# Expert tiles of 128 slots in place of 256 for the first three images of a deformable-convolution and mixture-of-experts block

## The chip, the cores and the metric

The kernel runs on one core of a Trainium2 chip. The metric is the device time of one execution in microseconds (us). Before the change it is 7743.53 us, the median of 9 runs between 7716.26 and 7766.05 us.

## The reference

The input is four images of 256 channels and 64 by 64 pixels, in 32-bit floats, as all arithmetic is.

```python
x = x + conv_ref(ln_c(x))        # three modulated deformable 3x3 convolutions, each with relu
t = to_tokens(x)                 # 4 images x 4096 tokens x 256
t = t + ffn_ref(ln_t(t))         # 8 experts, the two best of each token

# a deformable layer: an ordinary 3x3 convolution gives 9 offsets and masks a pixel,
# the input is sampled there bilinearly, and the 9 samples are contracted:
sampled = bilinear(x, ys, xs) * mask
out = einsum('bikhw,oik->bohw', sampled, wk) + b

# the experts:
probs = softmax(xf @ gate_w + gate_b);  top2_vals, top2_idx = top_k(probs, 2)
cw = zeros(N, 8).at[arange(N), top2_idx].add(top2_vals)
for e in range(8):
    out += cw[:, e] * (gelu(xf @ W1[e] + b1[e]) @ W2[e] + b2[e])   # 256 -> 512 -> 256
```

## The kernel before

The convolutions come as twelve stages, one for each layer and image (`run`, L1018). A stage is eight blocks of 512 pixels, and a block is nine taps, one for each place of the 3x3 kernel: 864 taps in all. For a tap, `samples` (L476) has POOL issue four indirect gathers of 128 rows (tile `g`), VectorE (DVE) blends each in two steps (L491, L496, tile `s`), and ScalarE (ACT) scales it (L499). `turn` (L503) has TensorE (PE) transpose the four results, eight transpositions into two PSUM tiles `tp` (L514), and ACT copy each half into `sT` (L517). `finish` (L523) then contracts `sT` with the tap's weights into `acc` (L537): four products of 512 columns. A 32-bit product is two passes on PE, and each pass is one record in the trace with a weight load of its own; a transposition is one pass.

Ten buffers hold `g` and eight hold `s`, so that POOL and DVE can run ahead of PE. The code calls `turn` two pairs of samples behind `samples`.

The experts of an image run beside later taps. `tokens` finds each token's two experts, `route` (L671) gives every token-and-expert pair a slot, sorted by expert, and fills the tables `tok` (which token is in a slot) and `wrow` (the rows of the weights of a tile). An expert's slots are rounded up to whole tiles. A `Group` is one image, or half of the last one: three groups of 39 tiles of 256 slots (`FT`, L36), and two of 23. `expert` (L806) does one tile in three pieces:

1. the tokens `zt`, 128 rows a DMA, are transposed into a `tp` tile (`ftp`, L821), and ACT copies it to `fzT` (L825);
2. the first products (`ph`, L837), in two halves that share one PSUM tile, and after each half two Gelus on ACT (`hT`, L847), a Gelu reading its bias from the weights' buffer;
3. the second products (`py`, L855). At the start of the next tile's first piece `products` (L864) adds the bias on DVE (`y`, L873) and stores the result by SP's queue.

`fetch` (L771) issues a tile's weights and then its tokens on POOL's queue. It is called in the third piece of the tile before (L851), behind the newest gather; while lanes are drained, in the second piece (L830). Of the weights there are two buffers, used in turn. The tiles are taken alternately from the first and the second half of a group (`order`, L86), so that each buffer walks the experts in order, and a request whose rows are those already in the buffer gets row numbers out of bounds: it is issued, but moves nothing (L733 to L737).

When a piece's turn comes is set by `Lane.go`: every tap gives a credit of one, and a piece of a tile costs a third of its group's pace (L1030), 5, 5, 2, 1.5 and 0 taps a tile. What is still left in the lanes after the last tap is drained.

This is the order in which the kernel's code names the work. A scheduler of the tile layer then orders the instructions of each engine, by a model of its own of when each can start; the engines run them in that order. `after` ties an instruction behind another one.

Of the kernel before, what the change touches and what calls it, by code (L numbers as in the profile page):

```python
# [33 lines left out]
HC = HID // P  # L34
FT_LOG = 8
FT = 1 << FT_LOG  # L36
FU = FT // P
GB = 10
# [34 lines left out]
class Group:  # L73


    def __init__(self, b, n0, n1):
        self.b, self.n0, self.n1 = b, n0, n1
        self.nm = f"{b}_{n0}"
        self.M = (n1 - n0) * TPB

        self.NF = 2 * self.M * P // FT + E - 1


        self.half = (self.NF + 1) // 2
        self.zt, self.acc, self.gy, self.sums, self.py = {}, [], [], [], None
        self.order = [s // 2 + s % 2 * self.half for s in range(self.NF)]  # L86
# [21 lines left out]
class Weave:  # L108
# [96 lines left out]
    def ffn_constants(self):  # L205
# [7 lines left out]
        ]  # L213
        nf = max(g.NF for g in self.groups)
        for g in self.groups:
            g.zd = self.dram.tile([g.M * P, C], F32, name=f"z_{g.nm}", tag=f"z_{g.nm}")
        self.ys = [
            self.dram.tile([nf * FT, C], F32, name=f"ys_{i}", tag=f"ys_{i}") for i in range(3)
        ]
# [40 lines left out]
        nc.vector.tensor_copy(self.row_f, row_i)  # L260
        assert FU * nf <= P
        self.token = cst.tile([P, NB * TPB], F32, name="token")
# [408 lines left out]
    def route(self, grp):  # L671

        nc, M, NF = self.nc, grp.M, grp.NF
        grp.slots = self.rt2.tile([P, 2, M], I32, tag="slots", bufs=3, name=f"slots_{grp.nm}")
        grp.tok = self.rt2.tile([P, FU * NF], I32, tag="tok", name=f"tok_{grp.nm}")
        grp.wrow = self.rt2.tile([P, NF], I32, tag="wrow", name=f"wrow_{grp.nm}")
# [19 lines left out]
        ni = small("ni", (P, E), I32)  # L696
        nc.vector.tensor_scalar(ni, slot[:, :, M - 1], float(FT - 1), None, ALU.add)
        nc.vector.tensor_scalar(ni, ni, FT_LOG, None, ALU.logical_shift_right)
        nt = small("nt", (P, E))
# [4 lines left out]
        nc.vector.tensor_tensor(off, end, nt, ALU.subtract)  # L704
        nc.vector.tensor_scalar(off, off, float(FT), None, ALU.mult)
        nc.vector.tensor_tensor(slot, slot, tot, ALU.subtract)
# [34 lines left out]
        for v, (op, k) in enumerate(((ALU.bitwise_and, P - 1), (ALU.logical_shift_right, 7))):  # L741
# [4 lines left out]
            grp.digits.append(df)  # L746
        grp.inv = self.ps1.tile([P, FU * NF], F32, tag="py", name=f"inv_{grp.nm}")

    def invert(self, grp, m):
# [3 lines left out]
        lo, hi = grp.digits  # L753
        n = FU * grp.NF
        for i in range(2):
# [15 lines left out]
    def fetch(self, grp, step):  # L771

        if self.w is None:
            self.w = [
                self.wt.tile([P, 2, WINN], F32, tag="wt", name=f"w_{i}").rearrange(
                    "p a b -> p (a b)"
                )
                for i in range(2)
            ]
        f = grp.order[step]  # L780
        self.nc.gpsimd.indirect_dma_start(  # L781
            out=self.w[step % 2][:, : W1N + W2N],
            out_offset=None,
            in_=self.ins["W"],
            in_offset=bass.IndirectOffsetOnAxis(ap=grp.wrow[:, f : f + 1], axis=0),
            bounds_check=E * P - 1,
            oob_is_err=False,
        )
        grp.zt[step] = []
        for u in range(FU):  # L790
            zt = self.ffn.tile([P, C], F32, tag=f"zt{u}", name=f"zt_{grp.nm}_{f}_{u}")
            j = FU * f + u
            self.nc.gpsimd.indirect_dma_start(  # L793
                out=zt,
                out_offset=None,
                in_=grp.zd,
                in_offset=bass.IndirectOffsetOnAxis(ap=grp.tok[:, j : j + 1], axis=0),
            )
            grp.zt[step].append(zt)

    def fetch_next(self, grp, step):
        if step + 1 < grp.NF:
            with self.after(self.gathered):
                self.fetch(grp, step + 1)

    def expert(self, grp, step):  # L806

        nc = self.nc
        if step == 0:
            self.fetch(grp, 0)  # L810
            yield
        self.products(grp)
        f = grp.order[step]
        nm = f"{grp.nm}_{f}"
        w = self.w[step % 2]
        w1, w2 = w[:, :W1N], w[:, W1N : W1N + W2N]
        zt = grp.zt.pop(step)
        tp = self.ps.tile([P, CC, FT], F32, tag="tp", name=f"ftp_{nm}")
        for u in range(FU):
            for c in range(CC):  # L820
                nc.tensor.transpose(  # L821
                    tp[:, c, u * P : (u + 1) * P], zt[u][:, c * P : (c + 1) * P], self.ident
                )
        zT = self.ffn.tile([P, CC, FT], F32, tag="zT", bufs=1, name=f"fzT_{nm}")
        nc.scalar.copy(zT, tp)  # L825
        yield

        beside = not self.draining
        if not beside:
            self.fetch_next(grp, step)  # L830
        hT = []
        for h0 in range(0, HC, 2):
            ph = self.ps1.tile([P, 2, FT], F32, tag="ph", name=f"ph_{nm}_{h0}")
            for h in range(2):
                for c in range(CC):
                    o = c * HID + (h0 + h) * P
                    nc.tensor.matmul(  # L837
                        ph[:, h, :],
                        lhsT=w1[:, o : o + P],
                        rhs=zT[:, c, :],  # L840
                        start=(c == 0),
                        stop=(c == CC - 1),
                    )
            ht = self.ffn.tile([P, 2, FT], F32, tag="hT", bufs=3, name=f"hT_{nm}_{h0}")
            for h in range(2):
                k = CC * HID + h0 + h
                nc.scalar.activation(ht[:, h, :], ph[:, h, :], AF.Gelu, bias=w1[:, k : k + 1])  # L847
            hT.append(ht)
        yield
        if beside:  # L850
            self.fetch_next(grp, step)  # L851
        py = self.ps1.tile([P, FU, C], F32, tag="py", name=f"py_{nm}")
        for u in range(FU):
            for h in range(HC):
                nc.tensor.matmul(  # L855
                    py[:, u, :],
                    lhsT=hT[h // 2][:, h % 2, u * P : (u + 1) * P],
                    rhs=w2[:, h * C : (h + 1) * C],
# [5 lines left out]
    def products(self, grp):  # L864
# [5 lines left out]
        grp.py = None  # L870
        y = self.ffn.tile([P, FU, C], F32, tag="y", name=f"y_{grp.nm}_{f}")
        with self.after(self.last):
            nc.vector.tensor_tensor(  # L873
                y, py, w2[:, HC * C :].unsqueeze(1).to_broadcast([P, FU, C]), ALU.add
            )
        nc.sync.dma_start(
            self.ys[grp.i % 3][f * FT : (f + 1) * FT, :].rearrange("(u p) c -> p u c", u=FU),
            y,
# [137 lines left out]
    def run(self):  # L1016
# [9 lines left out]
        last = self.B - 1  # L1026
        self.groups = [Group(b, 0, NB) for b in range(last)]
        self.groups += [Group(last, 0, NB // 2), Group(last, NB // 2, NB)]

        for i, (g, pace) in enumerate(zip(self.groups, (5.0, 5.0, 2.0, 1.5, 0.0))):  # L1030
            g.i, g.pace, g.last = i, pace, i + 1 == len(self.groups)
# [82 lines left out]
```

## Time and profile before

| | us |
|---|---|
| median of 9 runs | 7743.53 |
| profiled execution | 7722.13 |
| its span, first to last instruction | 7720.4 |
| PE busy | 6511.4 (84%) |
| DVE busy | 4878.4 (63%) |
| POOL busy | 4445.1 (58%) |
| ACT busy | 3464.2 (45%) |
| first products `ph`, PE busy, 2608 passes of 256 columns | 700.9 |
| second products `py`, PE busy, 2608 passes of 256 columns | 673.7 |
| weight requests on POOL, 163 | 177.2 |
| token requests on POOL, 326 | 330.7 |

The stretches that the text speaks of, in us from the span's start: 1236 to 2429 are taps with no tiles beside them, 2429 to 4075 hold the first group's 39 tiles, 4248 to 5879 the second's, 6091 to 6851 most of the third's, and from 7286 on no tap is left.

A row of a group of instructions reads: line, engine, operation, out<-in, shapes, count | busy us, mean ns of one | idle time of the engine just before them, with what ended it. "PEld" is PE's weight load, which overlaps the products. A row of waits reads: who waited <- for whom: us in total, times, longest us. The clock is the share of TensorE's clock that was granted.

### The profile page before, as it was taken

How to read it: one execution, taken by the hardware profiler on the slowest of the kernel's cores; microseconds unless marked ns; L12 is line 12 of the kernel's file. 1: busy time of each engine (PE TensorE's matmuls, PEld its weight loads, DVE VectorE, ACT ScalarE, POOL GpSimd, SP SyncE). 2: the span in 40 equal slices, each digit the busy share in tenths (PEclk: the TensorE clock that was granted, in tenths of full speed). 3: DMA queues.
4: the chain of work that ended last, by engine and by line, in shares of the span. 5: the costliest groups of instructions: out<-in, count | busy, mean ns of one | idle time of the engine just before them, and what ended most of it. 6: DMA issues, size and time to landing. Idle time of an engine off the chain costs nothing.

```text
span 7720.4 us, 89391 instructions
## 1 busy us (share of the span) xinstructions
PE 6511.4 (84%) x26756; PEld 3635.2 (47%) x26756; DVE 4878.4 (63%) x10829; ACT 3464.2 (45%) x7381; POOL 4445.1 (58%) x4245
## 2 busy tenths in 40 slices
PE   7888888888888888888887888888878788977887
PEld 3343333334444444545544444444444455644665
DVE  5666777767787666667667556666667654567421
ACT  4454444445554444445553434444544333444322
POOL 4554666655556656655546656665556655556543
PEclk8999999999999999999998989999989999989998
DMA  7887999988898888888778878888888877778643
GB/s 255 294 296 283 349 338 337 349 332 319 314 327 314 308 295 300 306 297 303 277 289 293 285 272 314 299 303 300 280 293 294 280 256 240 273 273 299 226 140 121
DMA packets 802369, 2223.77 MB, mean 288 GB/s; under 512 B 106776, under 2 KB 304920, under 8 KB 796128
## 3 DMA queue, kind: packets, MB, share of 16 engines
q0 software_dynamic: 551200, 1947.35, 70.9%
q1 hardware_dynamic: 250688, 270.69, 10.4%
q8 instruction: 217, 3.56, 0.2%
q14 instruction: 264, 2.16, 0.1%
HBM read 2160.68 MB, written 196.40 MB: 305 GB/s over the span
## 4 chain that ended last, share of the span: by engine, by line
PE 64%; ACT 10%; another core or an unknown queue 9%; issue 7%; DVE 4%; DMA 2%; POOL 1%; ACTq 0%; SPq 0%; DVEq 0%; POOLq 0%
PE acc L537 32%; PE tp L514 10%; PE ph L837 6%; PE py L855 6%; PE po L341 5%; ACT sT L517 4%; ACT s L499 3%; DVE g L491 2%; DVE s L496 1%; PE pm L355 1%; ACT hT L847 1%; PE tpv L315 1%; PE ftp L821 1%; ACT win L559 1%
## 5 line engine op out<-in xcount | busy, mean ns | idle before, releaser
L485 POOL DMA_INDIRECT g<-tab,idx x3456 | 3650.8, 1056 | 2531.6 <-DVE s L496 1199.9
L537 PE MATMUL acc<-sT,wk 128*128 128x512 f32 x6912 | 3543.9, 626 | 313.9 <-ACT sT L517 162.6
L491 DVE SCALAR_TENSOR_TENSOR g<-g,cf 128x512 f32<-128x512 f32 x3456 | 2560.6, 743 | 277.6 <-DMA g<-tab,idx 221.6
L496 DVE SCALAR_TENSOR_TENSOR s<-g,cf 128x256 f32<-128x256 f32 x3456 | 1662.6, 483 | 1376.0 <-PE tp L514 734.9
L517 ACT COPY sT<-tp 128x512 f32<-128x512 f32 x1728 | 1003.0, 585 | 2388.5 <-PE tp L514 1545.6
L514 PE MATMUL tp<-ident,s 128*128 128x128 f32 x6912 | 1312.7, 288 | 542.3 <-ACT s L499 319.8
L514 PEld LDWEIGHTS tp<-ident,s 128*128 128x128 f32 x6912 | 891.9, 146 | 1839.0 <-issue 948.0
L537 PEld LDWEIGHTS acc<-sT,wk 128*128 128x128 f32 x6912 | 1204.3, 200 | 1141.5 <-issue 839.8
L499 ACT ACTIVATE s<-s,cf 128x256 f32<-128x256 f32 x3456 | 1631.9, 507 | 233.1 <-DVE s L496 163.3
L837 PE MATMUL ph<-fzT,w 128*128 128x256 f32 x2608 | 700.9, 402 | 88.5 <-ACT fzT L825 32.2
L855 PE MATMUL py<-w,hT 128*128 128x256 f32 x2608 | 673.7, 398 | 116.3 <-ACT hT L847 78.6
L837 PEld LDWEIGHTS ph<-fzT,w 128*128 128x128 f32 x2608 | 493.7, 200 | 235.2 <-issue 82.3
L855 PEld LDWEIGHTS py<-w,hT 128*128 128x128 f32 x2608 | 487.6, 197 | 240.8 <-ACT hT L847 112.2
L847 ACT ACTIVATE hT<-ph,w 128x256 f32<-128x256 f32 x652 | 284.2, 470 | 606.1 <-PE ph L837 352.8
L793 POOL DMA_INDIRECT zt<-z,tok x326 | 330.7, 1014 | 162.9 <-issue 90.5
L781 POOL DMA_INDIRECT w<-in_W,wrow x163 | 177.2, 1087 | 390.3 <-issue 149.8
L341 PE MATMUL po<-win,wo 128*32 128x504 f32 (+1 forms) x2304 | 374.5, 612 | 3.4 <-ACT win L295 2.7
L896 POOL DMA_INDIRECT gy<-ys,slots x256 | 262.8, 1026 | 104.9 <-issue 71.0
L873 DVE TENSOR_TENSOR y<-py,w 128x512 f32<-128x512 f32 x163 | 111.9, 686 | 311.2 <-PE py L855 271.2
L911 DVE SCALAR_TENSOR_TENSOR ta<-gy,cw,ta 128x256 f32<-128x256 f32 x256 | 120.5, 480 | 114.1 <-DMA gy<-ys,slots 60.3
L318 ACT COPY hv<-tpv 128x512 f32<-128x512 f32 x192 | 112.6, 587 | 174.8 <-remote 75.0
L341 PE MATMUL po<-win_pre,wo 128*32 128x504 f32 (+1 forms) x1152 | 184.4, 598 | 0.0
(154 smaller groups left out, 3079.7 us busy)
## 6 DMA issues: line engine op xcount, KB each, us to landing
tab<-hv SPq DMA_DIRECT2D x768, 128.0 KB
g<-tab,idx POOLq DMA_INDIRECT x3456
ys<-y SPq DMA_DIRECT2D x163, 256.0 KB
wk<-in_conv_w SPq DMA_DIRECT2D x99, 256.0 KB
xc_pre<-in_x SPq DMA_DIRECT2D x32, 512.0 KB
xr_tok<-in_x SPq DMA_DIRECT2D x32, 512.0 KB
t<-t_tok SPq DMA_DIRECT2D x32, 512.0 KB
ta<-t SPq DMA_DIRECT2D x64, 256.0 KB
```

The lines of the kernel that those rows point to most:

```text
L341: nc.tensor.matmul(po[g * Q : (g + 1) * Q, :].rearrange("q (r w) -> q r w", w=W)[:, :, x0:x1], lhsT=self.wo[l][:, 3 * ky + kx, c, :], rhs= ...
L485: self.gathered = nc.gpsimd.indirect_dma_start(out=g.rearrange("p x s f -> p (x s f)"), out_offset=None, in_=self.table(*self.stages[i]), ...
L491: nc.vector.scalar_tensor_tensor(g[:, :, 0, :], g[:, :, 1, :], cf[:, j, 0:1], g[:, :, 0, :], ALU.mult, ALU.add,)
L496: self.last = nc.vector.scalar_tensor_tensor(s, g[:, 1, 0, :], cf[:, j, 1:2], g[:, 0, 0, :], ALU.mult, ALU.add)
L499: nc.scalar.activation(s, s, AF.Copy, scale=cf[:, j, 2:3])
L514: self.turned = nc.tensor.transpose(tp[:, c, u * P : (u + 1) * P], ss[u][:, c * P : (c + 1) * P], self.ident)
L517: nc.scalar.copy(self.sT[:, :, t0 * P : (t0 + 2) * P], tp)
L537: nc.tensor.matmul(acc[:, o, :], lhsT=self.wk[k][:, c, o * P : (o + 1) * P], rhs=sT[:, c, :], start=(k == 0 and c == 0), stop=(k == K - 1 ...
L793: self.nc.gpsimd.indirect_dma_start(out=zt, out_offset=None, in_=grp.zd, in_offset=bass.IndirectOffsetOnAxis(ap=grp.tok[:, j : j + 1], axi ...
L837: nc.tensor.matmul(ph[:, h, :], lhsT=w1[:, o : o + P], rhs=zT[:, c, :], start=(c == 0), stop=(c == CC - 1),)
L847: nc.scalar.activation(ht[:, h, :], ph[:, h, :], AF.Gelu, bias=w1[:, k : k + 1])
L855: nc.tensor.matmul(py[:, u, :], lhsT=hT[h // 2][:, h % 2, u * P : (u + 1) * P], rhs=w2[:, h * C : (h + 1) * C], start=(h == 0), stop=(h == ...
```

## The change

`Group` gets the number of 128-slot units of its tiles, `fu`: 1 for the first three groups and 2, as before, for the two halves of the last image. A group of the first three has 64 + 7 = 71 tiles of 128 slots in place of 32 + 7 = 39 of 256, that is 71 blocks of 128 slots in place of 78, and the paces go from 5, 5 and 2 taps a tile to 2.5, 2.5 and 1. In a small tile all four parts of the first products have 128 columns and lie in one PSUM tile, and their four Gelus follow them. The weights' request leaves `fetch` and becomes `weights`, called in the second piece of the tile itself, ahead of its first products.

```diff
-FT_LOG = 8
-FT = 1 << FT_LOG
-FU = FT // P
+FU = 2
...
-    def __init__(self, b, n0, n1):
+    def __init__(self, b, n0, n1, fu):
...
-        self.NF = 2 * self.M * P // FT + E - 1
+        self.fu, self.ft = fu, fu * P
+        self.NF = 2 * self.M // fu + E - 1
...
+    def weights(self, grp, step):
+        if step < grp.have or step >= grp.NF:
+            return
+        grp.have = step + 1
...
+        with self.after(self.gathered):
             self.nc.gpsimd.indirect_dma_start(
-                out=zt,
+                out=self.w[step % 2][:, : W1N + W2N],
...
     def expert(self, grp, step):
...
         if step == 0:
+            self.weights(grp, 0)
             self.fetch(grp, 0)
             yield
...
-        nc.scalar.copy(zT, tp)
+        nc.scalar.copy(zT[:, :, :ft], tp[:, :, :ft])
         yield
         beside = not self.draining
+        self.weights(grp, step)
         if not beside:
-            self.fetch_next(grp, step)
+            self.weights(grp, step + 1)
+            if step + 1 < grp.NF:
+                self.fetch(grp, step + 1)
         hT = []
-        for h0 in range(0, HC, 2):
-            ph = self.ps1.tile([P, 2, FT], F32, tag="ph", name=f"ph_{nm}_{h0}")
-            for h in range(2):
+        HQ = 4 // fu
+        for h0 in range(0, HC, HQ):
+            ph = self.ps1.tile([P, HQ, ft], F32, tag="ph", name=f"ph_{nm}_{h0}")
+            for h in range(HQ):
...
         yield
-        if beside:
-            self.fetch_next(grp, step)
+        if beside and step + 1 < grp.NF:
+            self.fetch(grp, step + 1)
...
-        self.groups = [Group(b, 0, NB) for b in range(last)]
-        self.groups += [Group(last, 0, NB // 2), Group(last, NB // 2, NB)]
-        for i, (g, pace) in enumerate(zip(self.groups, (5.0, 5.0, 2.0, 1.5, 0.0))):
+        self.groups = [Group(b, 0, NB, 1) for b in range(last)]
+        self.groups += [Group(last, 0, NB // 2, FU), Group(last, NB // 2, NB, FU)]
+        for i, (g, pace) in enumerate(zip(self.groups, (2.5, 2.5, 1.0, 1.5, 0.0))):
```

The other lines of the diff put `grp.fu` and `grp.ft` where `FU` and `FT` stood.

## The prediction

> **What bounds the kernel now.** First the page's busy shares and its chain of work that ended last.
>
> ```profile
> span 7720.4 us, 89391 instructions
> PE 6511.4 (84%) x26756; PEld 3635.2 (47%) x26756; DVE 4878.4 (63%) x10829; ACT 3464.2 (45%) x7381; POOL 4445.1 (58%) x4245
> ...
> PE 64%; ACT 10%; another core or an unknown queue 9%; issue 7%; DVE 4%; DMA 2%; POOL 1%; ACTq 0%; SPq 0%; DVEq 0%; POOLq 0%
> ```
>
> PE is busiest and carries 64% of the chain, ACT another 10%. Next the groups of instructions, to see whether the others run ahead.
>
> ```profile
> L485 POOL DMA_INDIRECT g<-tab,idx x3456 | 3650.8, 1056 | 2531.6 <-DVE s L496 1199.9
> L496 DVE SCALAR_TENSOR_TENSOR s<-g,cf 128x256 f32<-128x256 f32 x3456 | 1662.6, 483 | 1376.0 <-PE tp L514 734.9
> L837 PE MATMUL ph<-fzT,w 128*128 128x256 f32 x2608 | 700.9, 402 | 88.5 <-ACT fzT L825 32.2
> L847 ACT ACTIVATE hT<-ph,w 128x256 f32<-128x256 f32 x652 | 284.2, 470 | 606.1 <-PE ph L837 352.8
> L793 POOL DMA_INDIRECT zt<-z,tok x326 | 330.7, 1014 | 162.9 <-issue 90.5
> L781 POOL DMA_INDIRECT w<-in_W,wrow x163 | 177.2, 1087 | 390.3 <-issue 149.8
> ```
>
> They do: POOL idles for DVE to free a `g` buffer, and DVE for PE to free an `s` buffer. So PE, in step with ACT, sets the pace, and the cost of a product and PE's waits for ACT decide. The timeline gives the cost of a pass, from runs without a gap:
>
> ```profile
> 4006.09 2.74 PE L537 MATMUL acc<-sT,wk 128*128 128x512 f32 x6
> ...
> 4010.94 3.32 PEld L855 LDWEIGHTS py<-w,hT 128*128 128x128 f32 x16
> 4011.05 3.62 PE L855 MATMUL py<-w,hT 128*128 128x256 f32 x16
> ...
> 4016.22 1.04 PE L444 MATMUL tp_pre<-ident,h_pre 128*128 128x128 f32 x8
> ...
> 4025.14 0.97 PE L355 MATMUL pm<-strips,om 128*128 128x27 f32 x8
> ```
>
> Taking off the last one's own duration (0.59, 0.38, 0.27, 0.27): 512 columns cost (2.74-0.59)/5 = 0.43 us, 256 columns 0.216, a transposition of 128 columns 0.110, a product of 27 columns 0.100. The waits of PE in the first group's stretch (2429 to 4075) come last:
>
> ```profile
> PE tp L514 <- ACT s L499: 45.4, 38, 4.5
> ...
> PE acc L537 <- ACT sT L517: 12.7, 17, 2.6
> ...
> PE ph L837 <- ACT fzT L825: 7.0, 11, 0.7
> ```
>
> and, in the stretch without tiles (1236 to 2429), whose row of the same wait is five times as large:
>
> ```profile
> PE acc L537 <- ACT sT L517: 66.7, 68, 7.7
> ```
>
> This wait comes from order alone: where a tap's `acc` follows its last transposition directly, PE idles for the 0.585 us copy and two hand-overs, about 0.70. I listed the built program's order on PE, put the pass costs above on it, and summed by how much the work between those two falls short of 0.70: 171.7 us over all 864 taps, where the trace has 162.6; 13.7 against 12.7 in the first group, 20.0 against 16.0 in the second, 0 against under 1 in the third. So the listing can be used for the changed program.
>
> **The change, part by part.**
>
> *PE work.* A tile of 256 costs 4 x 0.110 + 16 x 0.216 + 16 x 0.216 = 7.36 us, times 39 is 287. A small tile has 2 transpositions, 16 passes `ph` of 128 columns and 8 passes `py` of 256. No row shows a product of 128 columns; it lies between 0.100 (27 columns, same weights) and 0.216. I take 0.110, the transposition's, because that row has the same columns and the 27-column row shows that the 190 ns weight load doesn't hold the stream above 0.100. Then 0.22 + 1.76 + 1.73 = 3.71, times 71 is 263: 24 us less a group, 71 for three, 75 at the granted clock of 0.95. The ends of the pass cost make it 105 less or 291 more.
>
> The Trainium skill ("TensorE: Matmul & The Clock Gate", Back-to-back issue gap) speaks against small column counts: it has 81 ns a product at 128 columns in streams of load and product, where the product alone takes 56. On these 32-bit passes that would be an estimated 0.155, and the whole sum 153 us higher; no row here has such a product, and the 27-column row stands against it.
>
> *PE's wait for `sT`.* The scheduler's order of the changed program differs. In the first group's taps `acc` follows the last transposition within 0.70 us in 122 taps of 198 (before 32), in the second's in 144 of 193 (40), in the third's in 56 of 68 (none). The shortfalls are 79.4, 94.3 and 37.7 us (13.7, 20.0, 0), over all taps 355.1 against 171.7. Scaled by 162.6/171.7 that is +174 us of PE waiting. The likely reason is that the scheduler takes each of 71 requests for a full load, so that in its model samples come late and PE has nothing to put between.
>
> *`ph` after `fzT`, `py` after the Gelus.* In the small tiles `ftp` stands far ahead of `ph`, and the wait that the rows show (7.0, and 14.9 in the second group) goes: -22. Between `ph` and `py` stands one `acc` product, 0.86 us, and the first Gelu needs about 0.4 (a 128x128 ACT copy takes 0.30, plus hand-overs): covered. By the listing -9; the rows `py` <- `hT` (14.6 and 29.7) would allow -44.
>
> *ACT.* Per small tile four Gelus of 0.30 (between half of 470 ns and all of it) and a copy of 0.45 (between 0.30 and 0.585), per large one four of 0.47 and 0.585: +21 us a group. After `ph` ACT needs 4 x 0.30 + 2 scalings of 0.51 (the mean of L499) = 2.2 us until PE's next transposition; PE meanwhile has `acc` and `py`, 2.6. Hidden; without that cover 63.
>
> *POOL, DVE, SP.* POOL gets 96 more weight requests of 1.09 us and 21 fewer token requests of 1.01: +83 us, hidden by its idle time for `g` buffers; DVE 7 us a group (71 of 0.48 against 39 of 0.686), hidden likewise; SP 96 more issues of 0.36, which nothing waits for. If POOL's cover is gone, in the third group, its share is 28 us. The DMAs move 21 blocks less each way, 5.5 of 2224 MB: nothing.
>
> *The weights, asked for later.* Of 163 requests 45 move data in the trace's packets, nine a group, landing 5 to 10 us after the issue. In the changed order `ph` stands on PE at the sample whose gather is the newest before the request. Before, that is so in the third group, and the products mostly start 18 to 30 us after the request, because POOL is that far ahead. Cost zero; without POOL's lead 27 loads of up to 8.5 us.
>
> *Sum.* -75 +174 -22 -9 = +68. The chain has PE and ACT at 74%, so I count +50, between that and all: 7772 on the profiled execution's 7722. The median of the runs stands 21 us above it: 7794.
>
> **The rivals.**
>
> 1. *Faster: the new wait only takes the place of another.* A PE that waits for `sT` gives ACT time, so the next transposition may wait less for `s`. The rows allow it: `tp` <- `s` is 45.4, 87.0 and 28.9 us in the three groups. Against it: the stretch without tiles has 66.7 us of `acc` <- `sT` and still 63.5 of `tp` <- `s`. If two thirds of the 174 are absorbed, -48 remains, and 74% of it is -36: 7708; with all absorbed 7640 to 7665. It decides once more than half is absorbed.
> 2. *Slower still: the weight requests hold POOL in the third group.* There the lead is thin:
>
> ```profile
> POOL w L781 <- ACT sT L517: 74.6, 14, 15.5
> POOL w L781 <- ACT s L499: 69.4, 13, 17.7
> ```
>
> POOL stood 197 us before 37 requests, for the buffer of two tiles ago, and gathers queue behind. With 71 such stands of 5.3 us and 0.5 us more work a tap, POOL needs 12.4 us a tap, where a tap now takes 11.2: +80, 7874. The distance to that buffer's last use stays 1.33 taps in code, which is why I don't expect it.
>
> 3. *Weight loads set the pass of 128 columns.* At 0.15 it costs 16 x 0.04 x 213 = 136: 7930.
> 4. *Weights come late*, POOL's lead lost: half of the loads exposed is 115 us: 7909.
> 5. *No difference*: the sum comes out between.
>
> **How the numbers follow.** A measurement tells this kernel from no change at about 0.2%, 15.5 us. The sum holds in 0.50 of the cases (its own range 7765 to 7840), rival 1 has 0.23, rival 2 0.10, rival 3 0.04, rival 4 0.03, no difference 0.10. So faster 0.23, same 0.10, slower 0.67. The range leaves out the all-absorbed part of rival 1 and rivals 3 and 4: 7690 to 7890.
>
> **What would show it.** In the changed kernel's profile: 4144 passes `ph`, of which 3408 of 128 columns spaced 0.110 us; 2440 `py`, 610 `ftp`; 259 requests for weights and still about 45 that move data. `acc` <- `sT` over the span near 335 us, in the first group near 75; `ph` <- `fzT` nearly gone; `py` <- `hT` small. I am wrong if `tp` <- `s` falls by as much as `acc` <- `sT` rises (rival 1), if POOL's idle time before `w` doubles and DVE waits for gathers in the third group (rival 2), if PE's passes `ph` stand 0.15 us or more apart (rival 3), or if PE waits for weights outside the drained end (rival 4).

## The result, and the profile after

The changed kernel takes 8268.08 us (median of 10 runs, 8245.51 to 8291.61) against 7741.07 us of the kernel before (31 runs): 1.068 times as long, 95% interval 1.0663 to 1.0696, or 527 us more. The forecast was 7794 us with a range from 7690 to 7890.

The page after, of the execution of 8249.6 us, first the busy shares and the chain of work that ended last:

```profile
PE 6655.4 (81%) x28082; PEld 3687.9 (45%) x28082; DVE 4898.1 (59%) x10925; ACT 3517.0 (43%) x7857; POOL 4459.7 (54%) x4320
...
PE 61%; ACT 12%; issue 9%; another core or an unknown queue 9%; DVE 3%; DMA 2%; POOL 0%; ACTq 0%; DVEq 0%; SPq 0%; POOLq 0%
```

PE's busy time is 144 us longer although it has less to do, and its share fell from 84% to 81%: no other engine became the bound, everybody idles more. The groups of instructions say where:

```profile
L538 PE MATMUL acc<-sT,wk 128*128 128x512 f32 x6912 | 3643.4, 636 | 494.1 <-ACT sT L518 302.1
...
L515 PE MATMUL tp<-ident,s 128*128 128x128 f32 x6912 | 1328.4, 291 | 677.9 <-ACT s L500 420.7
...
L886 DVE TENSOR_TENSOR y<-py,w 128x256 f32<-128x256 f32 (+1 forms) x259 | 122.0, 471 | 1723.2 <-PE py L867 1554.2
L867 PE MATMUL py<-w,hT 128*128 128x256 f32 x2440 | 663.2, 417 | 236.9 <-ACT hT L859 148.1
L859 ACT ACTIVATE hT<-ph,w 128x128 f32<-128x128 f32 (+1 forms) x1036 | 320.3, 386 | 1188.8 <-PE ph L849 626.2
...
L849 PE MATMUL ph<-fzT,w 128*128 128x128 f32 (+1 forms) x4144 | 613.0, 300 | 21.7 <-DMA w<-in_W,wrow 18.4
L802 POOL DMA_INDIRECT w<-in_W,wrow x259 | 277.8, 1073 | 442.8 <-DVE y L886 207.4
```

The counts are the forecast's: 4144 passes `ph`, 2440 `py`, 259 requests (of which 45 still move data, 5760 packets of 9,232 B in both traces). PE's wait for `sT` went from 162.6 us to 302.1, for `s` from 319.8 to 420.7, for the Gelus at `py` from 78.6 to 148.1, and DVE stands 1554 us at `y` where it stood 271.

By stretches, taking the time from tap to tap: the first group's 197 taps take 1906 us in place of 1643, the second's 193 take 1892 in place of 1633, the third's 68 take 761 in place of 764. The 166 taps ahead of the first group take 1187 and 1195. So all of the loss lies beside the first two groups' tiles, 263 and 259 us, and none beside the third's.

**Two kinds of chip.** The experiments did not run on the chip of the forecast. On some chips the kernel before takes 7741 to 7749 us ("first kind"), on others 6822 to 6828 ("second kind"), so each ratio below is to the kernel before on the same chip. On the second kind the changed kernel loses less: 1.0433 (1.0415 to 1.0450), 291 us.

> The changed kernel as it is, on the chip of the other experiments: the kernel before takes 6822 us there (7741 on the first), so every comparison needs both there. If the loss is of the kernel's order alone, its ratio is the 1.068 of the first chip; if stalls of TensorE's clock have made it larger there, it is less, 1.03 to 1.05.

> The kernel before as it is, for its trace on this chip: no change.

It was the case of the smaller ratio. PE's waits on the second kind, whole run, before:

```profile
PE tp L514 <- ACT s L499: 198.1, 306, 5.1
PE acc L537 <- ACT sT L517: 152.0, 232, 2.8
PE py L855 <- ACT hT L847: 36.1, 62, 6.9
...
PE ph L837 <- ACT fzT L825: 27.5, 41, 1.3
```

and after:

```profile
PE acc L538 <- ACT sT L518: 335.2, 497, 2.5
PE tp L515 <- ACT s L500: 296.9, 579, 5.2
...
PE ph L849 <- DMA w<-in_W,wrow: 22.2, 9, 8.4
PE py L867 <- ACT hT L859: 16.4, 25, 6.7
```

Here the picture is clean: more waits for ACT at `acc` and at `tp`, fewer at `ph` and `py`. These rows undercount. Each wait starts only at the modelled end of the pass before it, some 0.165 us after the next pass could have started (a transposition is shown with 0.273 us of its own, while the next one starts 0.107 us after it). So I took PE's passes from start to start and subtracted each pass's own cost (0.427 us for 512 columns, 0.213 for 256, 0.107 for 128 or fewer; between two `po` all of it). What is left over, by the pass that it stands ahead of, in us:

| | second kind: before | after | difference | first kind: difference | forecast |
|---|---|---|---|---|---|
| passes' own cost | 5663 | 5596 | -67 | -63 | -75 |
| ahead of `acc` | 343 | 582 | +239 | +273 | +174 |
| ahead of `tp` | 414 | 589 | +175 | +213 | 0 |
| ahead of `ph` | 112 | 74 | -38 | -79 | -22 |
| ahead of `py` | 93 | 66 | -27 | +155 | -9 |
| ahead of others | 182 | 194 | +12 | +30 | |
| sum | 6807 | 7102 | +295 | +529 | +68, of which 74% counted |

The spans differ by 296.5 and 529.2 us, so the table holds all of it.

### The profile page after: what moved, and what is told of

Same layout as the page of the kernel before. It is cut to its first block, busy times and chain, and to the rows that moved or that the text cites. A ratio compares the mean times of both kernels' runs of the same rounds, so it can differ in the third digit from the quotient of the medians.

```text
span 8249.6 us, 93615 instructions
## 1 busy us (share of the span) xinstructions
PE 6655.4 (81%) x28082; PEld 3687.9 (45%) x28082; DVE 4898.1 (59%) x10925; ACT 3517.0 (43%) x7857; POOL 4459.7 (54%) x4320
## 4 chain that ended last, share of the span: by engine, by line
PE 61%; ACT 12%; issue 9%; another core or an unknown queue 9%; DVE 3%; DMA 2%; POOL 0%; ACTq 0%; DVEq 0%; SPq 0%; POOLq 0%
PE acc L538 30%; PE tp L515 10%; PE py L867 7%; PE ph L849 6%; ACT sT L518 5%; PE po L342 5%; ACT s L500 4%; DVE g L492 1%; DVE s L497 1%; PE pm L356 1%; PE ftp L826 1%; PE tpv L316 1%; ACT win L560 1%; ACT hT L859 1%
## 5 line engine op out<-in xcount | busy, mean ns | idle before, releaser
L486 POOL DMA_INDIRECT g<-tab,idx x3456 | 3600.3, 1042 | 2999.6 <-DVE s L497 1644.1
L538 PE MATMUL acc<-sT,wk 128*128 128x512 f32 x6912 | 3643.4, 636 | 494.1 <-ACT sT L518 302.1
L515 PE MATMUL tp<-ident,s 128*128 128x128 f32 x6912 | 1328.4, 291 | 677.9 <-ACT s L500 420.7
L886 DVE TENSOR_TENSOR y<-py,w 128x256 f32<-128x256 f32 (+1 forms) x259 | 122.0, 471 | 1723.2 <-PE py L867 1554.2
L867 PE MATMUL py<-w,hT 128*128 128x256 f32 x2440 | 663.2, 417 | 236.9 <-ACT hT L859 148.1
L859 ACT ACTIVATE hT<-ph,w 128x128 f32<-128x128 f32 (+1 forms) x1036 | 320.3, 386 | 1188.8 <-PE ph L849 626.2
L849 PEld LDWEIGHTS ph<-fzT,w 128*128 128x128 f32 x4144 | 568.1, 197 | 164.6 <-issue 123.7
L849 PE MATMUL ph<-fzT,w 128*128 128x128 f32 (+1 forms) x4144 | 613.0, 300 | 21.7 <-DMA w<-in_W,wrow 18.4
L802 POOL DMA_INDIRECT w<-in_W,wrow x259 | 277.8, 1073 | 442.8 <-DVE y L886 207.4
L342 PE MATMUL po<-win,wo 128*32 128x504 f32 (+1 forms) x2304 | 398.5, 622 | 14.3 <-ACT om L351 6.3
L780 POOL DMA_INDIRECT zt<-z,tok x305 | 303.0, 993 | 154.2 <-issue 76.8
L830 ACT COPY fzT<-ftp 128x256 f32<-128x256 f32 (+1 forms) x259 | 107.0, 413 | 184.9 <-PE ftp L826 109.2
```

Source lines behind the costliest of these rows:

```text
L342: nc.tensor.matmul(po[g * Q : (g + 1) * Q, :].rearrange("q (r w) -> q r w", w=W)[:, :, x0:x1], lhsT=self.wo[l][:, 3 * ky + kx, c, :], rhs= ...
L486: self.gathered = nc.gpsimd.indirect_dma_start(out=g.rearrange("p x s f -> p (x s f)"), out_offset=None, in_=self.table(*self.stages[i]), ...
L515: self.turned = nc.tensor.transpose(tp[:, c, u * P : (u + 1) * P], ss[u][:, c * P : (c + 1) * P], self.ident)
L538: nc.tensor.matmul(acc[:, o, :], lhsT=self.wk[k][:, c, o * P : (o + 1) * P], rhs=sT[:, c, :], start=(k == 0 and c == 0), stop=(k == K - 1 ...
L780: self.nc.gpsimd.indirect_dma_start(out=zt, out_offset=None, in_=grp.zd, in_offset=bass.IndirectOffsetOnAxis(ap=grp.tok[:, j : j + 1], axi ...
L849: nc.tensor.matmul(ph[:, h, :], lhsT=w1[:, o : o + P], rhs=zT[:, c, :ft], start=(c == 0), stop=(c == CC - 1),)
```

## The experiments

Three theories stood at the start. Y: DVE, which works in order, is held at `y` until PE has done `py`, and its lead becomes too short. O: PE's order, `acc` directly behind its tap's last transposition, as the forecast had it, but dearer. T: the small tiles cost by themselves, by their 96 more requests and shorter pieces. A fourth, G, came out of the runs.

**What the trace seemed to say: DVE is held at `y` (theory Y).** In the built order DVE's `y` stands 6 samples past the first pass of its `py` in the first two groups, before 15.7 and 17.5. Two runs moved this, one each way, and left PE's order all but as it was.

In `expert` of the changed kernel (`small_late_y`; while lanes are drained, `y` stays in the first piece):

```diff
             yield
-        self.products(grp)
+        if self.draining:
+            self.products(grp)
...
+        self.products(grp)
         py = self.ps1.tile([P, fu, C], F32, tag="py", name=f"py_{nm}")
```

and in `expert` of the kernel before (`big_early_y`):

```diff
         grp.py = (f, py, w2)
+        self.products(grp)
```

> The changed kernel with one thing moved: the addition of the bias (tile `y` on DVE) is named in the third piece of the next tile, ahead of its `py`, in place of the first piece. In the built order `y` then stands 10.5 samples past its `py` in the first and the second group (6.0 and 6.1 in the changed kernel, 15.7 and 17.5 before); PE's order is all but the same (shortfall of `acc` behind `sT` 342 us against 355). Theory Y (DVE, which works in order, is held at `y` until PE has done `py`, so its lead over PE is too short): most of the 527 us come back, 7780 to 7900, and DVE's idle time for `py` falls from 1554 us to under 700. Theory O (PE's order, that is the products directly behind their last transposition, at some 2.9 us for each us of shortfall): 8230. Theory T (the small tiles' own work and their 96 more requests): 8268.

> The kernel before with one thing moved: `y` is named directly behind its `py`, in the same piece. In the built order `y` stands 7.7, 10.0 and 5.2 samples past `py` in the three groups (15.7, 17.5 and 7.3 before); PE's order is the same (shortfall 175 us against 172). Theory Y: slower, by 80 to 350 us (7820 to 8090), and DVE's idle time for `py` rises from 311 us to over 700. Theory O and theory T: no change, 7741 within 16.

Measured, both on the second kind: 1.0414 (1.0397 to 1.0432) against the changed kernel's 1.0433, and 0.9932 (0.9916 to 0.9949), 45 us less where none of the three theories had a gain. DVE's waits, first of the changed kernel as it is and with late `y`:

```profile
DVE y L886 <- PE py L867: 1113.4, 193, 13.6
DVE s L497 <- PE tp L515: 162.8, 231, 4.3
```

```profile
DVE s L497 <- PE tp L515: 620.4, 474, 8.9
DVE g L492 <- DMA g<-tab,idx: 428.8, 336, 7.7
DVE y L890 <- PE py L871: 227.9, 41, 11.4
```

and of the kernel before as it is and with early `y`:

```profile
DVE s L496 <- PE tp L514: 447.7, 490, 7.4
...
DVE y L873 <- PE py L855: 217.8, 36, 10.9
```

```profile
DVE y L874 <- PE py L855: 785.3, 136, 15.4
DVE s L496 <- PE tp L514: 177.8, 260, 4.5
```

The stand at `y` went from 1113 us to 228 and nothing was won; it went from 218 to 785 and 45 us were won (why there is a gain is not settled). Theory Y falls: the largest new row of the page is time in which DVE would have waited anyway, at `s`.

**The two halves of the change.** `small_old_w` puts the request back into `fetch`, ahead of the tokens:

```diff
+        self.weights(grp, step)
         f = grp.order[step]
         grp.zt[step] = []
...
         beside = not self.draining
-        self.weights(grp, step)
```

`big_new_w` has tiles of 256 slots in the changed kernel, so that only the request is late:

```diff
-        self.groups = [Group(b, 0, NB, 1) for b in range(last)]
+        self.groups = [Group(b, 0, NB, FU) for b in range(last)]
...
-        for i, (g, pace) in enumerate(zip(self.groups, (2.5, 2.5, 1.0, 1.5, 0.0))):
+        for i, (g, pace) in enumerate(zip(self.groups, (5.0, 5.0, 2.0, 1.5, 0.0))):
```

> The changed kernel with the weights' request back in its old place, ahead of the token requests in the piece that fetches for the next tile. The built order has `y` 10.0, 10.6 and 3.8 samples past `py`, and PE's shortfall at `acc` is 253 us (355 in the changed kernel, 172 before). Theory Y: 7760 to 7880. Theory O: 7741 + 2.9 x 81 = 7980. Theory T: 8268. If the late request itself is what costs (weights that come late), all of the loss goes: 7741 or less.

> Tiles of 256 slots and the old paces everywhere, but the weights asked for in the new place: the other half of the change alone. The built order has `y` 12.2, 12.2 and 7.3 samples past `py`, PE's shortfall is 250 us. Theory Y: `y` is no hindrance, what is left is PE's waits by my sum, 7741 + 0.74 x 78 = 7800. Theory O: 7741 + 2.9 x 78 = 7967. Theory T: 7741. Weights that come late: 7900 or more, with PE waiting at `ph`.

Measured: 1.0244 (1.0227 to 1.0261) and 0.9987 (0.9978 to 0.9997). Theory O in its first form, so much for each us of shortfall at `acc`, fails: with the same shortfall of 250 us one run loses 162 us and the other nothing. Asked late, large tiles lose nothing; with the request in its old place, small tiles lose a good half of what the change loses. It takes both parts for the whole.

**The loads, or the order that they bring?** Three edits leave loads out. In all three most tiles use the weights of another expert. `small_skip` keeps every instruction and their order, but lets all but the first two requests of a group move nothing, which leaves out 35 of the 45 loads (in `route`):

```diff
-        nc.vector.tensor_tensor(same[:, 1:], ex[:, 1:], ex[:, : NF - 1], ALU.is_equal)
+        nc.vector.tensor_tensor(same[:, 1:], ex[:, 1:], ex[:, : NF - 1], ALU.is_ge)
```

`small_tiny_w`, and `big_tiny` on the kernel before, keep the requests, but those of steps past the first two are small, which gives another order:

```diff
-                out=self.w[step % 2][:, : W1N + W2N],
+                out=self.w[step % 2][:, : W1N + W2N] if step < 2 else self.w[step % 2][:, :4],
...
-                in_=self.ins["W"],
+                in_=self.ins["W"] if step < 2 else self.ins["W"].rearrange("r (a b) -> (r a) b", b=4),
```

`small_two_w` leaves them out (in `weights`):

```diff
+        if step > 1:
+            return
         with self.after(self.gathered):
```

> The changed kernel with one comparison exchanged (is_equal for is_ge), so that every request past the first two of a group gets row numbers out of bounds and brings nothing: the change of expert is left out, most tiles use weights of the wrong expert. Every engine's order is that of the changed kernel. If the loss lies in the order: the ratio to the kernel before stays at the changed kernel's 1.043, less 0.003 for PE's waits for weights (22 us). If it lies in the loads themselves (weights that come late, DMA time): 0.98 to 1.01.

> The changed kernel with all 259 requests in their new places, but every request past the first two of a group brings only 4 columns a row in place of 2308, so the products of most tiles use weights of the wrong expert: part of the computation is left out. The scheduler then gives PE nearly the order of before: shortfall at `acc` 179 us (355 in the changed kernel, 172 before); `y` stands as in the changed kernel, 6.2 samples past `py`. Theory O (PE's order and what follows from it): the loss is gone, ratio to before 0.985 to 1.005. Theory Y (DVE held at `y`): the ratio stays within 0.01 of the changed kernel's. Theory T (the small tiles' work and 96 more requests): it stays as well.

> The changed kernel with only the first two requests of each group; the rest is left out, and with it the change of expert, so the products of most tiles use weights of the wrong expert. Shortfall at `acc` 161 us, `y` 7.4 samples past `py`. Against the run with 4 columns a row it has 249 requests less on POOL. Theory O: the same ratio as that run, within 0.005. If the requests on POOL and their waits for the buffer are what costs: 0.02 to 0.04 below that run.

> The kernel before (large tiles, requests in the old place) with only 4 columns a row in every request past the first two of a group; most tiles use weights of the wrong expert, so part of the computation is left out. Its order has a shortfall at `acc` of 152 us (172 before) and ACT 1.98 and 0.43 samples ahead (0.57 and 0.20 before). If the cheap request helps by the order it brings, large tiles gain less than small ones, since they have 163 requests in place of 259 and had the better order: 0.985 to 1.0 on a chip of the second kind, and small tiles with 4 columns (0.979) are no slower. If what helped there was the load left out (45 loads in both kernels), the gain here is as large as there, 441 us or 6.5 %.

Measured: `small_skip` 1.0674 (1.0652 to 1.0697) on the first kind, the changed kernel's 1.068: the 35 loads left out cost nothing that can be measured, and the loss is there with the order alone. On the second kind `small_tiny_w` 0.9787 (0.9770 to 0.9804), `small_two_w` 0.9707 (0.9691 to 0.9723) and `big_tiny` 0.9875 (0.9856 to 0.9894). So small tiles with the order that cheap requests bring are 441 us faster than with the order that full ones bring, and 63 us faster than large tiles with cheap requests, near the 67 us less of PE's own work. That is below the 0.985 expected. The step from 4 columns to none gives 54 us, 0.008, between the 0.005 and the 0.02 expected; the orders of these two differ as well, so what the requests on POOL cost by themselves isn't settled beyond that. Large tiles gain 0.0125 and not 6.5%, so the gain of the small ones lies in the order.

So what does the order contain beyond `acc`? The listing has a second thing that I had not counted. At each tile's first Gelu I took the scalings of samples that stand before it on ACT, less the samples whose transpositions stand before the tile's last `ph` on PE: what ACT has ready when it may go on. In a large tile, whose `ph` and Gelus come in two halves, I took each half against its own last `ph`, and the mean of the two. First and second group, beside the ratios:

| run (second kind) | ready at the Gelus | shortfall at `acc`, us | ratio |
|---|---|---|---|
| changed kernel | 0.11, 0.01 | 355 | 1.0433 |
| `small_late_y` | 0.11, 0.01 | 342 | 1.0414 |
| `small_old_w` | 1.07, 0.80 | 253 | 1.0244 |
| kernel before | 1.55, 1.01 | 172 | 1 |
| `big_new_w` | 1.33, 1.11 | 250 | 0.9987 |
| `big_tiny` | 3.37, 1.34 | 152 | 0.9875 |
| `small_tiny_w` | 2.90, 2.00 | 179 | 0.9787 |
| `small_two_w` | 4.96, 2.90 | 161 | 0.9707 |

The table does not order small tiles against large ones: `small_old_w` and `big_new_w` stand close in both columns and 0.026 apart in the ratio. The mean hides that in `big_new_w` the first half stands at 0.26 and 0.03, nearly as empty as the changed kernel's; but while PE does the second half, ACT scales on, and that half stands at 2.41 and 2.21. A small tile has no second half.

In the changed order `ph` stands on PE behind transpositions that the code names after it. ACT works in order and waits at the Gelus until PE has done that `ph`; with nothing scaled ahead it then walks the taps that follow in step with PE. The timeline of the changed kernel on the second kind (start, duration, engine; idle before in brackets; only lines of PE and ACT are shown) shows it:

```profile
2300.19 0.91 ACT L500 ACTIVATE s<-s,cf 128x256 f32<-128x256 f32 x2
...
2300.76 0.83 PE L515 MATMUL tp<-ident,s 128*128 128x128 f32 x4 [0.28 <-ACT s L500]
...
2301.62 0.59 ACT L518 COPY sT<-tp 128x512 f32<-128x512 f32 x1 [0.53 <-PE tp L515]
...
2302.26 1.98 PE L538 MATMUL acc<-sT,wk 128*128 128x512 f32 x4 [0.68 <-ACT sT L518]
...
2304.08 1.95 PE L849 MATMUL ph<-fzT,w 128*128 128x128 f32 x16
...
2306.07 1.14 ACT L859 ACTIVATE hT<-ph,w 128x128 f32<-128x128 f32 x4 [3.86 <-PE ph L849]
...
2307.08 0.93 ACT L500 ACTIVATE s<-s,cf 128x256 f32<-128x256 f32 x2
...
2308.45 0.60 PE L515 MATMUL tp<-ident,s 128*128 128x128 f32 x4
```

Two scalings, the transpositions that waited for them, the copy that waited for those, the products that waited for the copy; and in the 3.86 us in which ACT waits for `ph` it scales nothing, because the Gelus stand first in its order. Where the price falls can be read from the traces: in the first two groups, where two to seven samples have been transposed since a tile's `ph`, PE loses 386 us ahead of `tp` and `acc` in the changed kernel, and 45 us in the run that comes next; beyond the seventh sample the two are nearly alike (105 and 132 us).

**Undoing one thing: `ph` back where the code has it (theory G).**

In `turn`, and in `expert` (`small_tp`):

```diff
-                self.turned = nc.tensor.transpose(
-                    tp[:, c, u * P : (u + 1) * P], ss[u][:, c * P : (c + 1) * P], self.ident
-                )
+                with self.after(self.tiled):
+                    self.turned = nc.tensor.transpose(
+                        tp[:, c, u * P : (u + 1) * P], ss[u][:, c * P : (c + 1) * P], self.ident
+                    )
...
-                    nc.tensor.matmul(
+                    self.tiled = nc.tensor.matmul(
                         ph[:, h, :],
```

> The changed kernel with one tie: a tap's transpositions (`tp`) may not stand ahead of first products `ph` that the code names before them. In the built order `ph` then stands where the code has it, and a tile's Gelus on ACT stand 4.1 and 4.2 scaled samples ahead of PE in the first two groups (0.11 and 0.01 in the changed kernel, 1.55 and 1.01 before); PE's shortfall at `acc` falls on the way from 79 and 94 us to 31 and 40. Theory G (ACT, which works in order, is held at the Gelus until PE has done `ph` and has no scaled sample ahead then): nearly all of the loss goes, ratio 0.980 to 1.000 on a chip of the second kind (changed kernel 1.043), 0.985 to 1.015 on one of the first (1.068). If only the shortfall at `acc` counts, at 1.25 us each: 1.017 and 1.03 to 1.04.

Measured: 0.9898 (0.9881 to 0.9914) on the second kind, 367 us below the changed kernel: as much as the whole loss and 71 us more, with small tiles, 259 late requests and `y` where the change has it (6.7 samples past `py`). PE's waits:

```profile
PE acc L539 <- ACT sT L519: 202.3, 321, 2.7
PE tp L516 <- ACT s L500: 152.6, 292, 5.0
...
PE py L868 <- ACT hT L860: 27.9, 35, 5.5
```

From start to start the passes take 252 us less ahead of `tp`, 159 less ahead of `acc` and 27 more ahead of `py` than in the changed kernel. Its timeline at a tile, again only PE and ACT:

```profile
2311.25 2.05 PE L850 MATMUL ph<-fzT,w 128*128 128x128 f32 x16
...
2313.14 0.60 PE L516 MATMUL tp<-ident,s 128*128 128x128 f32 x4
...
2313.34 1.14 ACT L860 ACTIVATE hT<-ph,w 128x128 f32<-128x128 f32 x4 [5.27 <-PE ph L850]
...
2313.76 1.99 PE L868 MATMUL py<-w,hT 128*128 128x256 f32 x8
```

ACT waits for `ph` as before (872 us over the run, 888 in the changed kernel), but now the next transpositions have their samples and follow `ph` at once. The tie also lowers the shortfall at `acc` over the run from 355 us to 215, so this run does not part the two; the next ones bear on that. The tie was not put alone on the kernel before, so the run undoes the loss but does not say which tile is the better one.

**Forcing the rest of the order.** One tie puts `acc` behind the newest transposition (`small_tie_pe`, in `finish`):

```diff
-                nc.tensor.matmul(
-                    acc[:, o, :],
...
+                with self.after(self.turned):
+                    nc.tensor.matmul(
+                        acc[:, o, :],
```

A second, in `small_tie` and `small_tie_2` and, on the kernel before, in `big_tie` and `big_tie_2`, puts ACT's copy to `sT` behind the newest scaling; `small_tie_tp` and `big_tie_tp` have the tie at `tp` besides.

```diff
-            nc.scalar.activation(s, s, AF.Copy, scale=cf[:, j, 2:3])
+            self.scaled = nc.scalar.activation(s, s, AF.Copy, scale=cf[:, j, 2:3])
...
-        nc.scalar.copy(self.sT[:, :, t0 * P : (t0 + 2) * P], tp)
+        with self.after(self.scaled):
+            nc.scalar.copy(self.sT[:, :, t0 * P : (t0 + 2) * P], tp)
```

> The changed kernel with the `acc` products tied behind the newest transposition, as the code names them; the scheduler may no longer put them directly behind their own tap's. Shortfall at `acc` 0 in the whole program (355 us in the changed kernel); ACT scales 1.1 and 0.5 samples ahead of PE's need in the first two groups (0.30 and 0.11 in the changed kernel, 0.57 and 0.20 before, 1.41 and 0.54 in the run with 4 columns a row). Theory O: PE's wait for `sT` (335 us, 497 times, each some 0.165 us dearer than the idle row says) goes and part of that for `s`: 6650 to 6800, ratio 0.975 to 0.996. If PE only waits for `s` in its place: 1.02 to 1.04.

> As the run before, and each copy to `sT` on ACT is tied behind the newest scaling of a sample, so that ACT has 4 samples scaled ahead of PE's need throughout. Theory O: both waits of PE go, in the stretches without tiles too: 6450 to 6650, ratio 0.945 to 0.975, `acc` <- `sT` and `tp` <- `s` under 100 us together but for waits for late samples. If the lead on ACT is taken from elsewhere (copies wait for samples that come late): above the run with PE's tie alone.

> The kernel before with both ties. Theory O: its own 152 us of `acc` <- `sT` and 198 us of `tp` <- `s` go: 6500 to 6650, ratio 0.953 to 0.975; and with the order made equal, the small tiles are no slower than the large ones: the run with small tiles and both ties takes as long or up to 75 us less. If the small tiles cost by themselves (259 requests, shorter pieces): this run is 50 us or more below that one.

> Small tiles with both ties once more, hoped for on a chip of the second kind (6822 us before, on which TensorE's results never come later than the profile's modelled ends). If the 251 us by which it stands above large tiles with both ties are such late ends (some 100 to 150 us a group more on the chip of the first kind), the two are within 40 us of each other here. If the small tiles cost by themselves (259 requests, 71 tiles' hand-overs), 100 us or more remain.

> Large tiles with both ties, beside the run before it, on the same chip: 6500 to 6650 us on a chip of the second kind, 0.977 of the kernel before on one of the first.

> The same tie together with the two others (small tiles). Gelus 4.5 samples ahead (0.82 and 0.34 with the two ties alone), shortfall 0. Theory G: the two ties alone left 80 us to the large tiles because ACT still stood at the Gelus with nothing ahead; that goes, and small tiles are at or below large ones with both ties (0.966 on the second kind, 0.977 on the first): 0.948 to 0.964 and 0.955 to 0.980. If the small tiles cost by themselves: 0.975 and 1.00 or more.

> Large tiles (the kernel before) with the same three ties. Their Gelus stood 3.3 and 2.3 samples ahead with two ties already, 4.8 and 2.7 now. Theory G: little is left to gain, within 0.006 of the run with two ties (0.966 and 0.977), and above the small tiles by 0 to 75 us of PE's work.

| | first kind | second kind |
|---|---|---|
| small, tie at `acc` | 1.0524 (1.0497 to 1.0550) | |
| small, `acc` and `sT` | 1.0105 (1.0085 to 1.0126) | 0.9777 (0.9759 to 0.9794) |
| large, `acc` and `sT` | 0.9769 (0.9751 to 0.9786) | 0.9659 (0.9637 to 0.9681) |
| small, `acc`, `sT` and `tp` | | 0.9670 (0.9654 to 0.9686) |
| large, `acc`, `sT` and `tp` | | 0.9775 (0.9759 to 0.9791) |

The tie at `acc` alone takes the shortfall from 355 us to nothing and brings back only 0.016 of the 0.068: the shortfall that I had forecast from is the smaller part. It leaves ACT with 0.71 and 0.20 samples at the Gelus, and PE now waits at `tp`, where the changed kernel's row on this kind was 420.7 us:

```profile
PE tp L515 <- ACT s L500: 671.3, 426, 16.4
```

From start to start PE loses 615 us less ahead of `acc` than in the changed kernel and 340 more ahead of `tp`, 74 more ahead of `py` and 124 more elsewhere. That is nearer the case that the expectation named second, that PE only waits for `s` in its place.

With the second tie small tiles still stood 81 us above large ones (251 on the first kind), with 0.82 and 0.34 samples at the Gelus against 3.3 and 2.3. The tie at `tp` brings small tiles to 4.5 and some 75 us down, with a shortfall of nothing in both runs, level with the best large ones. These, the kernel before with two ties, have the lowest time that I measured and beat both kernels: 6594 us on the second kind, 7570 on the first; small tiles with all ties, 6600 us, can't be told from them. So the shortfall alone does not make the loss: without it most of the loss stays, and `big_new_w` has 250 us of it and loses nothing. The runs point at what ACT has ready for the larger part; how the loss divides between the two is not settled, since `small_tp` moves both.

Several expectations missed. The tie at `acc` alone came out as said above, not at 0.975 to 0.996. Small tiles with two ties stand just above their range (0.9777 against 0.975), and their 81 us above large ones lie between the two cases named, under 40 and over 100. Small tiles with all ties are not below large ones with two (0.9670 against 0.9659), though PE has less to do. Large tiles lose 79 us by the tie at `tp` in place of staying level; part of that is PE's wait for the Gelus at `py`, 73 us in place of 25, since `ph` moves and `py` doesn't. From start to start the passes of small tiles with all ties cost 85 us less than those of large ones with two, and lose 59 more ahead of `ph`, 12 ahead of `py` and 34 ahead of passes other than `acc` and `tp`, so PE's gain goes into other waits; what brings those is not settled.

## Why the prediction was wrong

- **The step that failed is *ACT*, put at nothing: "Hidden; without that cover 63".** I had asked whether PE has something to do while ACT does the Gelus and two scalings (2.2 us against 2.6), and it has: in the timeline `tp` at 2308.45 starts without a wait. What I had not asked is where ACT stands afterwards. It leaves every tile with nothing scaled ahead, and the price falls in the taps between: 579 waits of PE for `s` in place of 306, 175 us from start to start (213 on the first kind), forecast as 0. Forcing `ph` to its place in the code removes it. I had written that `ph` stands late in the changed order, but asked of it only whether the weights would have landed.
- *PE's wait for `sT`*, +174: right in the row (152 to 335 us on the second kind, +183, and "near 335" had been forecast for the span), 239 from start to start. That the row hits 335 is in part luck: the forecast was for the first kind, where the row is 302.1 and the cost from start to start 273 more. I had scaled the shortfall to the idle row, which leaves out some 0.165 us a wait.
- *The sum at 74%*: wrong. PE's waits, taken from start to start, add up to the whole of the span, so nothing of them is hidden; counted in full, and with the 65 us that the row leaves out, the forecast would have been 83 us nearer.
- *PE work*, -75: -67 measured. On these passes 16 of 128 columns take 1.95 us, the last one's own duration 0.28, so they stand 0.111 us apart. Rival 3 is out. The Trainium skill ("TensorE: Matmul & The Clock Gate", Back-to-back issue gap) had led to an estimate of 0.155; the measurement decides against it here.
- *`ph` and `py`*: `ph` <- `fzT` went as forecast. On the second kind `py` did too, a little better. On the first kind `py` costs 155 us more, which no step had.
- *POOL, DVE, SP, weights asked later*, all costed at nothing: right for the engines and the loads, but not for the order. Asked late, small tiles lose 136 us more than asked in the old place (7119 against 6983 us, second kind), and large tiles nothing. POOL's idle time before `w` went from 390.3 to 442.8 us, the third group lost nothing on the first kind and 23 us on the second (rival 2), PE waits 22.2 us for weights there, 26.9 before (rival 4), and `small_skip` shows that the loads cost nothing that can be measured. The 1554 us of DVE at `y` are hidden as well.
- *Rival 1*, that the wait for `sT` takes the place of that for `s`, went the other way: both rose. The exchange that it spoke of shows in the run with the tie at `acc` alone, from `acc` to `tp`.
- *The first kind's own part*, 527 less 291: no step of the forecast had it. On this chip ACT and DVE often start well after the modelled end of the pass that they wait for; the waits table calls the releaser "remote". More than 1.5 us late, they are some 35 to 40 in each of the two groups before (120 to 140 us a group) and 50 to 70 after (230 to 280 us). On the second kind there is none in either kernel. Some four fifths of those after have a record of half the clock within 2 us. One of them:

```profile
2906.80 1.89 PE L867 MATMUL py<-w,hT 128*128 128x256 f32 x8
...
2914.32 0.42 DVE L886 TENSOR_TENSOR y<-py,w 128x256 f32<-128x256 f32 x1 [3.11 <-remote]
...
2918.66 0.58 ACT L518 COPY sT<-tp 128x512 f32<-128x512 f32 x1 [10.19 <-remote]
...
2919.98 0.69 PE L515 MATMUL tp<-ident,s 128*128 128x128 f32 x2 [8.69 <-ACT s L500]
...
2921.34 3.78 PE L538 MATMUL acc<-sT,wk 128*128 128x512 f32 x4 [0.68 <-ACT sT L518]
```

`py` should have ended at 2908.7, and `y` starts at 2914.3; then PE idles 8.69 us, and its next four products take 3.78 us, where 1.98 is usual. Half-clock records add up to 947 us before and 1194 after on the first kind, 226 and 260 on the second. Every idle stretch of PE above 4 us ends in such a record: 58 before and 86 after on the first kind, 6 and 6 on the second; of those of 1 to 2 us it is 25 of 154 after on the first kind. So longer idle stretches bring more half clock, and that this makes a loss of order larger on this chip fits these numbers, but no run tests it. The Trainium skill ("TensorE: Matmul & The Clock Gate", What's actually happening) has the rate halved after an idle window of about 3.4 us; the products after the 8.69 us agree. It does not say why PE's results come late on one kind of chip, nor does any run here, and so the split of the 236 us between late results and half clock stays open.

## What to carry to other kernels

When a change moves work in an engine's order, list for each engine that works in order how far ahead it stands at the place where it must wait, not only whether that one wait is covered: an engine that leaves the wait with nothing ready pays at every hand-over that follows. The largest new row of idle time (here 1554 us of DVE at `y`) need not be the loss; move it alone, both ways, before believing it. And where a scheduler orders by its own model, a request that mostly moves nothing seems to be a full load to that model still (the order changed when the requests were made small); here a tie to the code's order was worth 367 us, and the work saved 67.

## What the runs showed of the hardware

- The same program takes 13% longer on one kind of chip than on another (7741 against 6822 us), with granted clocks of 0.939 and 0.984, and a change of the order is 1.8 times as dear there (527 against 291 us).
- A request whose rows are all out of bounds shows in the trace as 128 packets of 4 bytes, 9 ns each (`small_skip` has 35 such requests more and 4480 such packets more); 96 more of them cost POOL 1.07 us each, hidden. Of the 45 that bring 1.18 MB each, 35 could be left out without a gain (1.068 and 1.0674).
- A wait in the rows of waits is some 0.165 us shorter than what it costs PE from start to start, because a pass's modelled end lies that much past the earliest start of the next one (0.273 less 0.107 us for a transposition, 0.59 less 0.427 for 512 columns).
